# A second convolution in column halves, with three gate buffers in the room of a closed stage

## The chip, the cores and the metric

The kernel runs on one core of one Trainium2 chip. The metric is the device time of one launch in microseconds (us). Lower is better. A profiled execution leaves a trace, whose span runs from its first to its last instruction.

## What is computed

The input x is 2 images of 256 channels by 64 x 64, in fp32. Two layers follow each other.

```python
# layer 0: attention over all 4096 positions, 8 heads of 32 channels, and a mask
q, k, v = 1x1 convolutions of x
fuse    = softmax(q k^T / sqrt(32)) v
x       = (Wf [x; fuse] + bf) * m + x * (1 - m)
# layer 1: channel gate, window attention, spatial gate
x = x * sigmoid(relu(x ca_w1 + b) ca_w2 + b)
x = x + window_attention(x)            # windows of 8 x 8, 4 heads
x = x with its 256 channels shuffled (4 groups)
y = relu(bn1(conv7x7(x, sa_w1)))       # 64 groups: 4 channels in, 1 out
y = bn2(conv7x7(y, sa_w2))             # 64 groups: 1 channel in, 4 out
out = x * sigmoid(y)
```

The change is in the last convolution and in the gate after it.

## The kernel before

**Prologue.** Pools mk, w0, st0, x0 and cw (line 372) hold masks, weights, staging tiles, all of x and the convolution weights while q, k and v are projected and written to memory. v comes last: a matmul from x0 (line 470), a copy into a tile vst of st0 (478), two stores by POOL (483).

**Attention.** `pipeline` walks through 1024 slots of 128 keys. For each slot, `scores` multiplies k and q (631) and lets ScalarE (ACT) write exp into a tile e (641); `products` multiplies v and e on TensorE (PE, 660) and adds e up on VectorE (DVE, 662). k and v are loaded by SyncE (SP) in pieces (558, 560), two ahead, behind q (565) at the start; x and the mask for the first stage follow them (571, 574). Everything else is hung into these slots: `later` and `stages` hold steps with due times, and `stage(b, c)` does the rest of layer 0 and the window attention for 8 image rows, step by step, up to the rows xs in memory (980), which the convolution reads. The order of all engines is the order of the program (`manual_schedule`).

**Pools.** `arm` opens f, x, g and w (the stages' tiles) first, then `pipeline` opens conv, e (8 tiles e of 8 KB a partition and 3 sums of 8 KB), and kv and q, one after the other from the same end of the on-chip memory. kv and q are closed when the last slot is done, and a pool "late" takes their room. f, x, g and w stay open to the end.

**Convolution.** A 7 x 7 convolution is done as 7 matmuls over shifted columns d, with the rows of a block and their neighbours on the partitions, and banded weights that are prepared in memory. Rows are cut into three blocks (line 43) of up to 30. Four groups of channels make a unit u; there are 16 units. `items` (989) are 24 pieces of work: units 0 to 7 of image 0, units 2 to 7 of image 1, units 8 to 15 of both images at once, and units 1 and 0 of image 1. Items with one image have 3 x 64 = 192 columns, those with both 384. For item k,

- `conv1(k)` (1037) multiplies 4 x 7 times: all 128 rows, 32 weight columns for each of four groups (c1, 1046), then ReLU on ACT into y (1054);
- `conv2(k)` (1061) takes 32 rows of y, one strip for each j, with 128 weight columns, 4 x 7 times (c2, 1070). Its four results lie in two PSUM tiles of two banks, of which there are three in all. ACT takes tanh into z (1080) and z/4 + 1/4 (1086);
- `gate(k)` (1089) multiplies z by x on DVE (1092) and stores it: 12 stores for each image (1105), half from POOL and half from SP; items 4 to 7, after the stages, from POOL alone; the last item from ACT and SP. Then SP loads the rows of item k + 4 (1025) and the next weights (1018).

`convolve` hands items out in the order conv1(k + 1), conv2(k), gate(k), as a generator. The first ones are drawn while the last stage runs: `next(conv)` comes between its steps (1206 to 1209). Then `staged` is set, and the rest runs by itself. z has two buffers, each for two images (1077), from the pool "late".

The weights of c2 are `w[r, d]` from a view "p (m d) -> p d m": neighbouring columns stand 7 elements, 28 bytes, apart. A matmul on fp32 appears in the profile as two instructions, with a weight load each.

Of the kernel before, what the change touches and what calls it, by code (L numbers as in the profile page):

```python
# [10 lines left out]
F32 = mybir.dt.float32  # L11
# [6 lines left out]
B, C, H, W = 2, 256, 64, 64  # L18
N = H * W
P = 128  # L20
# [17 lines left out]
KS, PAD = 7, 3  # L38
# [2 lines left out]

RB = 30
BLOCKS = ((0, 0, 24), (17, 24, 40), (34, 40, 64))
NG = C // 4
UG = 4
UQ = UG // 4
NU = NG // UG
UW = UG * KS
# [7 lines left out]
def conv_seq_kernel(ctx: ExitStack, tc: tile.TileContext, a, out):  # L56
    nc = tc.nc
# [13 lines left out]
    def psum2(name):  # L71
        return ps["pair"].tile([P, 2, CH], F32, tag="s", name=name)
# [48 lines left out]

    x_s = dram.tile([B, len(BLOCKS), P, NG, WP], F32, name="xs")

# [42 lines left out]
    def prepare(mk, cwp):  # L166
# [19 lines left out]
        rows = 32 + 4  # L186
        bn1 = cwp.tile([rows, NG, 5], F32, name="bn1")
        nc.gpsimd.dma_start(
            bn1, a["bn1"].rearrange("g s o -> (g s o)").partition_broadcast(rows)
        )  # L190
        raw1 = cwp.tile([rows, NG, KS], F32, name="raw1")
        src = a["sa_w1"].rearrange("(h g) k (y x) -> h k y g x", h=2, y=KS)
# [20 lines left out]
        for i in range(4):  # L213
            for j in range(4):
                nc.gpsimd.dma_start(
                    raw2[KS * j : KS * j + KS, :, i, :], src[i % 2, i // 2, j]
                )
        m1 = cwp.tile([rows, NG, KS], F32, name="m1")
        nc.gpsimd.memset(m1, 0.0)
# [5 lines left out]
        for b in range(B):  # L225
            for n, r in ((0, 0), (len(BLOCKS) - 1, 31)):
                for q in range(4):
                    nc.gpsimd.dma_start(
                        x_s[b, n, 32 * q + r].rearrange("(p g) w -> p (g w)", g=2),
                        zero[0 : NG // 2, 0 : 2 * WP],  # L230
                    )
# [140 lines left out]
    with (  # L372
# [48 lines left out]
        for i, (b, c) in enumerate(chunks):  # L421
            load_chunk()
            x = xs0[i]
            sq = st0.tile([P, 2 * KC, CH], F32, tag="sq", name=f"sq_{b}_{c}")
            tops = st0.tile([P, 2 * KC, CH // 4], F32, tag="top4", name=f"top4_{b}_{c}")
            for n, w in (("q", wq), ("k", wk)):
                s = psum2(f"{n}0_{b}_{c}")
                for g in range(KC):
                    for kc in range(KC):
                        rhs = x[:, kc, :]  # L430
                        if n == "q":
# [5 lines left out]
                            start=(kc == 0),  # L437
                            stop=(kc == KC - 1),
# [26 lines left out]
        for i, (b, c) in enumerate(chunks):  # L465
            s = psum2(f"v0_{b}_{c}")
            sv = s.rearrange("p a (t o) -> p (a t) o", t=2)
            for m in range(4):
                for kc in range(KC):
# [4 lines left out]
                        start=(kc == 0),  # L474
                        stop=(kc == KC - 1),
# [21 lines left out]
            elif i == 2:  # L497
# [3 lines left out]
                for oc in range(KC):  # L501
                    for kc in range(KC):
# [4 lines left out]
                            start=(kc == 0),  # L507
                            stop=(kc == KC - 1),
# [11 lines left out]


    def pipeline(arm, shifted, pools):
        fp, xpool, gp, wp, avp, ctx_conv = pools
        cpool = ctx_conv.enter_context(tc.tile_pool(name=f"conv{arm}", bufs=1))

        ep = ctx_conv.enter_context(tc.tile_pool(name=f"e{arm}", bufs=EB))
# [1 line left out]
        att = ExitStack()  # L528
# [193 lines left out]
        def stage(b, c):  # L722
# [241 lines left out]
            for oc in range(KC):  # L964
# [4 lines left out]
                )  # L969
                for n, (x0, _, _) in enumerate(BLOCKS):  # L970

# [16 lines left out]

        items = [(u, (0,)) for u in range(EARLY)] + [(u, (1,)) for u in range(2, EARLY)]
        items += [(u, (0, 1)) for u in range(EARLY, NU)] + [(1, (1,)), (0, (1,))]  # L990
        staged = []

        def convolve():
            nb = len(BLOCKS)

# [13 lines left out]
            def load_w(u):  # L1009
                if u >= NU:  # L1010
                    return
                n = 2 * 32 * UW
                if u == 0:
                    t = cpool.tile([P, n], F32, name=f"w{arm}{u}")
                else:
                    t = ep.tile([P, HG, CH], F32, tag="e", name=f"w{arm}{u}")
                    t = t.rearrange("p h n -> p (h n)")[:, 0:n]
                nc.sync.dma_start(t, w_s[u])
                ws[u] = t
# [41 lines left out]
            def conv2(k):  # L1061
                u, images = items[k]
                n = nb * len(images)
                y = ys.pop(k)
                w = ws[u][:, 32 * UW :].rearrange("p (m d) -> p d m", d=KS)
                tiles = [psum2(f"c2{arm}{k}_{hh}") for hh in range(2)]
                for d in range(KS):
                    for j in range(4):
                        r = slice(32 * j, 32 * j + 32)
                        nc.tensor.matmul(  # L1070
                            tiles[j // 2][:, j % 2, 0 : n * W],
                            w[r, d],
                            y[r, 0:n, d : d + W],
                            start=(d == 0),
                            stop=(d == KS - 1),
                        )
                z = pool.tile([P, 4, B * nb * W], F32, tag="z", name=f"z{arm}{k}", bufs=2)
                z = z[:, :, 0 : n * W]
                for hh in range(2):
                    nc.scalar.activation(  # L1080
                        z[:, 2 * hh : 2 * hh + 2, :],
                        tiles[hh][:, :, 0 : n * W],
                        AF.Tanh,
                        scale=0.5,
                    )
                nc.scalar.activation(z, z, AF.Copy, bias=0.25, scale=0.25)  # L1086
                return z.rearrange("p j (n x) -> p j n x", x=W)

            def gate(k, z):
# [10 lines left out]
                for m, b in enumerate(images):  # L1100
                    for n, (x0, r0, r1) in enumerate(BLOCKS):
                        for i in range(4):
# [20 lines left out]
            load_rows(3)  # L1123
            load_w(0)
            pool = yield
            for _ in range(4):
                load_w(weights.popleft())
            conv1(0)
            yield
            for k, (u, images) in enumerate(items):  # L1130
                while len(xs) <= k + 1 < len(items):
                    if not more():
                        yield
                conv1(k + 1)
                yield
                more()
                z = conv2(k)
                yield
                more()
                gate(k, z)  # L1140
                if xcs or k + 4 < EARLY:
                    load_rows(k + 4)

                if weights and (weights[0] <= 1 + EB or k >= EARLY):
                    load_w(weights.popleft())
# [25 lines left out]
        for i, (b, c, g, m) in enumerate(slots):  # L1171
            now[0] = i
            if (b, c, g, m) == (B - 1, NCHUNK - 1, 0, 0):
                for _ in banded:
                    pass
                conv = convolve()
                next(conv)
            if m % PB == 0:
                load_piece(i // PB + AHEAD)
            if g == KC - 1 and m == 0:  # L1180
                nxt = (b, c + 1) if c + 1 < NCHUNK else (b + 1, 0)
                if nxt[0] < B:
                    load_q(*nxt)
            rest = scores(i + 2) if i + 2 < len(slots) else None
            products(i)
            if rest:
                rest()
            if g == KC - 1 and m == NMB - 1:
                late = EB + 5 if (b, c) == (0, 0) else 0
                at(DN + 6 + late, lambda b=b, c=c: stages.append(stage(b, c)))  # L1190
            run_later()
            if i % 5 == 1:
                next(banded, None)
            if i % 4 == 0:
                run_stages()
# [11 lines left out]
        while stages:  # L1207
            if run_stages():
                next(conv)
        staged.append(True)  # L1210
        for _ in conv:
            pass
        psum.close()
# [1 line left out]

    def arm(name, shifted):
        with (
            tc.tile_pool(name=f"f{name}", bufs=1) as fp,
            tc.tile_pool(name=f"x{name}", bufs=1) as xpool,
            tc.tile_pool(name=f"g{name}", bufs=1) as gp,  # L1220
            tc.tile_pool(name=f"w{name}", bufs=1) as wp,
            tc.tile_pool(name=f"av{name}", bufs=1, space=PSUM) as avp,
            ExitStack() as ctx_conv,
            tc.manual_schedule(),
        ):
            pipeline(name, shifted, (fp, xpool, gp, wp, avp, ctx_conv))

    safe = nc.values_load(flag[0:1, 0:1], min_val=0, max_val=1)
    with tc.If(safe > 0) as cond:
        arm("a", False)  # L1230
    with cond.Else():
        arm("b", True)
# [65 lines left out]
```

## Time and profile before

Three runs took 3001.16, 3001.5 and 3005.74 us. The page of the profiled execution has these numbers; its own time beside the span is not given.

| | |
|---|---|
| median of the runs | 3001.5 us |
| span of the profiled execution | 3002.6 us |
| PE busy | 2969.7 us (99%) |
| DVE busy | 2502.6 us (83%) |
| ACT busy | 2480.2 us (83%) |
| POOL busy | 267.0 us (9%) |
| c2: matmul instructions, mean | 1344, 438 ns |
| c2: matmul busy | 100.2 us |
| first and last c2 | 2779.7 and 2988.2 us |
| stores of the output by POOL | 210 of 569 ns |
| ACT's first activation of z waiting for stores | 69.2 us in all |

Busy time is the time in which an engine has at least one instruction running, so that matmuls side by side count once. PEld is the load of weights, which overlaps matmuls. "SPq" is the issue of a DMA by SyncE. The idle time that a line names is that of the engine just before the instruction, and the arrow shows what ended it.

### The profile page before, as it was taken

Reading aid. Unit: us, or ns where it says so; the run is one execution under the profiler, and the core shown is the slowest. Engines: PE = TensorE matmul, PEld = TensorE weight load, DVE = VectorE, ACT = ScalarE, POOL = GpSimd, SP = SyncE. Lnnn points to the kernel's source line nnn. Section 1 sums busy time; section 2 is a strip of 40 time slices with the busy share of each in tenths; the row PEclk is TensorE's granted clock in tenths of the full one; section 3 lists DMA queues with packets and bytes.
Section 4 is the critical chain, followed back from the end, with each engine's and each line's share of the span. In section 5 each row is a group of like instructions: output and inputs, shape, how many; then the busy total and the mean of one; then the engine's idle time right before and its main releaser. Section 6 shows DMA issues by size and latency. Waiting matters only on the chain.

```text
span 3002.6 us, 61009 instructions
## 1 busy us (share of the span) xinstructions
PE 2969.7 (99%) x25226; PEld 1016.9 (34%) x25226; DVE 2502.6 (83%) x1348; ACT 2480.2 (83%) x4151; POOL 267.0 (9%) x470
## 2 busy tenths in 40 slices
PE   9999999999999999999999999999999999999997
PEld 3552323222223222223222222322222222223775
DVE  3349999899999999998999999999999899999211
ACT  5569889898989898988989898989898898988433
POOL 8010000000000000000000000000000000000356
PEclk9999999999999999999999999999999999999999
DMA  8544321222242323232222222222323222422464
GB/s 245 201 172 159 119 69 52 77 64 71 55 77 62 80 59 80 62 70 69 67 68 64 69 58 71 62 71 61 78 65 71 68 68 67 106 62 82 143 194 105
DMA packets 223951, 266.03 MB, mean 89 GB/s; under 512 B 113384, under 2 KB 130108, under 8 KB 223408
## 3 DMA queue, kind: packets, MB, share of 16 engines
q1 hardware_dynamic: 200880, 231.47, 26.8%
q0 software_dynamic: 18416, 27.87, 4.6%
q8 instruction: 201, 3.29, 0.5%
q10 hardware_dynamic: 4368, 2.70, 0.3%
q14 instruction: 86, 0.70, 0.1%
HBM read 213.49 MB, written 66.13 MB: 93 GB/s over the span
## 4 chain that ended last, share of the span: by engine, by line
PE 95%; DVE 2%; DMA 1%; POOL 1%; ACT 1%; SPq 0%; issue 0%; DVEq 0%; ACTq 0%; POOLq 0%
PE sa L631 36%; PE ava L660 33%; PE qka L804 4%; PE hya L733 4%; PE c2a L1070 2%; PE q L433 2%; PE vwa L890 2%; PE k L433 2%; PE opa L954 2%; PE c1a L1046 2%; PE v L470 2%; DVE suma L662 1%; PE dna L683 1%; POOL out_dram L1105 1%; PE sca L838 1%; DMA out_dram<-za 1%
## 5 line engine op out<-in xcount | busy, mean ns | idle before, releaser
L662 DVE TENSOR_TENSOR suma<-suma,ea 128x2048 f32<-128x2048 f32 x960 | 2199.0, 2291 | 87.9 <-ACT ea L641 1.8
L641 ACT ACTIVATE ea<-sa 128x512 f32<-128x512 f32 (+1 forms) x3072 | 2044.4, 744 | 89.0 <-PE sa L631 38.0
L631 PE MATMUL sa<-qa,ka 32*128 32x512 f32 x8192 | 1191.9, 639 | 1.5 <-ACT vst L478 1.2
L660 PE MATMUL ava<-ea,va 128*32 128x512 f32 x8192 | 1091.1, 605 | 0.3 <-ACT fa L670 0.3
L631 PEld LDWEIGHTS sa<-qa,ka 32*128 32x128 f32 x8192 | 338.6, 183 | 755.7 <-ACT ea L641 686.3
L660 PEld LDWEIGHTS ava<-ea,va 128*32 128x32 f32 x8192 | 161.5, 108 | 779.0 <-issue 752.1
L980 POOL DMA_DIRECT2D xs<-xo x94 | 65.9, 708 | 2541.1 <-DVE xo L965 2540.9
L1105 POOL DMA_DIRECT2D out_dram<-za x210 | 117.8, 569 | 80.2 <-DVE za L1092 56.5
L804 PE MATMUL qka<-ua,qkv_w 128*128 128x512 f32 x256 | 118.4, 605 | 0.0
L1092 DVE TENSOR_TENSOR za<-za,xla 128x768 f32<-128x768 f32 (+1 forms) x16 | 21.7, 1359 | 113.6 <-ACT za L1086 82.5
L662 DVE TENSOR_TENSOR suma<-ea,ea 128x2048 f32<-128x2048 f32 x32 | 73.1, 2284 | 51.3 <-ACT ea L641 51.3
L1070 PE MATMUL c2a<-yca,wa 32*128 32x192 f32 (+1 forms) x1344 | 100.2, 438 | 7.5 <-ACT za L1080 7.5
L1080 ACT ACTIVATE za<-c2a 128x384 f32<-128x384 f32 (+1 forms) x48 | 26.2, 595 | 95.5 <-DMA out_dram<-za 69.2
L452 DVE TENSOR_REDUCE top<-sq 128x512 f32<-128x2048 f32 x16 | 36.6, 2286 | 79.8 <-ACT sq L446 79.8
L741 ACT ACTIVATE ta<-hya,bf 128x512 f32<-128x512 f32 x32 | 20.3, 684 | 95.3 <-PE hya L733 89.2
L1070 PEld LDWEIGHTS c2a<-yca,wa 32*128 32x128 f32 x1344 | 91.3, 315 | 18.2 <-issue 9.6
L859 ACT ACTIVATE ewa<-ewa,mxwa 128x64 f32<-128x64 f32 x256 | 85.2, 346 | 1.5 <-DVE mxwa L850 1.5
L817 ACT ACTIVATE qka<-qka,qkv_b 128x512 f32<-128x512 f32 x64 | 40.5, 683 | 41.8 <-PE qka L804 41.6
L745 DVE TENSOR_TENSOR ta<-ta,mca 128x512 f32<-128x512 f32 x32 | 22.1, 689 | 62.9 <-ACT ta L741 62.9
L804 PEld LDWEIGHTS qka<-ua,qkv_w 128*128 128x128 f32 x256 | 46.0, 189 | 71.3 <-issue 46.1
L433 PE MATMUL q<-x,WqT 128*128 128x512 f32 x128 | 61.7, 627 | 5.4 <-DMA WqT<-in_WqT_dram 5.4
L890 PE MATMUL vwa<-qkv_w,ua 128*128 128x256 f32 x256 | 59.5, 386 | 0.0
(137 smaller groups left out, 1516.8 us busy)
## 6 DMA issues: line engine op xcount, KB each, us to landing
ka<-ks SPq DMA_DIRECT2D x256, 256.0 KB
va<-vs SPq DMA_DIRECT2D x256, 256.0 KB
wa<-ws SPq DMA_DIRECT2D x17, 896.0 KB
ws<-zeros SPq DMA_DIRECT2D x16, 896.0 KB
xs<-xo POOLq DMA_DIRECT2D x78, 140.0 KB, 6.5
xla<-xs SPq DMA_DIRECT2D x24, 420.0 KB
x<-in_x_dram SPq DMA_DIRECT2D x16, 512.0 KB
qs<-qst SPq DMA_DIRECT2D x16, 512.0 KB
```

Source lines behind the costliest of these rows:

```text
L433: nc.tensor.matmul(s[:, g, :], w[:, kc, g * P : (g + 1) * P], rhs, start=(kc == 0), stop=(kc == KC - 1),)
L631: nc.tensor.matmul(heads[j], k[r, cols], q[r, g, :], start=True, stop=not shifted)
L641: nc.scalar.activation(e[:, h, :], tile, AF.Exp, scale=SCALE0)
L660: nc.tensor.matmul(av[r, :], v[:, m % PB, r], e[:, j, :], start=start, stop=stop)
L662: nc.vector.tensor_add(total, first[0] if m == 1 else total, e)
L733: nc.tensor.matmul(s[:, oc, :], wf[:, kc, oc * P : (oc + 1) * P], f[:, kc - KC, :] if half else xw[kc], start=(kc == 0), stop=(kc == 2 * K ...
L804: nc.tensor.matmul(s[:, j, :], wqkv[:, kc, o : o + P], u[:, kc, :], start=(kc == 0), stop=(kc == KC - 1),)
L859: nc.scalar.activation(e[:, n, :], e[:, n, :], AF.Exp, bias=mx[:, n : n + 1], accum_out=rs[:, n : n + 1],)
L890: nc.tensor.matmul(sv[:, t, :], u[:, kc, t * P : (t + 1) * P], wqkv[:, kc, 2 * C : 3 * C], start=(kc == 0), stop=(kc == KC - 1),)
L980: eng.dma_start(x_s[b, n, p + r0 : p + r1].rearrange("r g w -> g r w"), xo[64 * h : 64 * h + 64, oc, r0 - WS * c : r1 - WS * c, :],)
L1070: nc.tensor.matmul(tiles[j // 2][:, j % 2, 0 : n * W], w[r, d], y[r, 0:n, d : d + W], start=(d == 0), stop=(d == KS - 1),)
L1105: engines[stores % len(engines)].dma_start(dst[b, i, r0:r1, UG * u : UG * u + UG, :], z[p + r0 : p + r1, :, nb * m + n, :],)
```

## The change

The stationary operand of c2 is split into two halves of 64 columns. Each half is a matmul of its own, into the lower or upper 64 partitions of the same PSUM bank, with the same moving columns of y.

The four pools of the stages are opened on the right side of the memory, in the same order, and the others on the left without them below. When the last stage is done they are closed, and a pool "gate" is opened there. z has three buffers. While stages run it is taken from "late", with room for one image; after that from "gate", with room for two.

```diff
+HALVES = (slice(0, 64), slice(64, 128))
...
-        staged = []
+        staged, zpool = [], []
...
                 for d in range(KS):
                     for j in range(4):
                         r = slice(32 * j, 32 * j + 32)
-                        nc.tensor.matmul(
-                            tiles[j // 2][:, j % 2, 0 : n * W],
-                            w[r, d],
-                            y[r, 0:n, d : d + W],
-                            start=(d == 0),
-                            stop=(d == KS - 1),
-                        )
-                z = pool.tile([P, 4, B * nb * W], F32, tag="z", name=f"z{arm}{k}", bufs=2)
+                        for o in HALVES:
+                            nc.tensor.matmul(
+                                tiles[j // 2][o, j % 2, 0 : n * W],
+                                w[r, d, o],
+                                y[r, 0:n, d : d + W],
+                                start=(d == 0),
+                                stop=(d == KS - 1),
+                            )
+                size = B * nb * W if staged else nb * W
+                z = zpool[-1].tile([P, 4, size], F32, tag="z", name=f"z{arm}{k}", bufs=3)
...
             pool = yield
+            zpool.append(pool)
...
         staged.append(True)
+        stg.close()
+        zpool.append(att.enter_context(tc.tile_pool(name=f"gate{arm}", bufs=1, side="right")))
         for _ in conv:
             pass
...
         with (
-            tc.tile_pool(name=f"f{name}", bufs=1) as fp,
-            tc.tile_pool(name=f"x{name}", bufs=1) as xpool,
-            tc.tile_pool(name=f"g{name}", bufs=1) as gp,
-            tc.tile_pool(name=f"w{name}", bufs=1) as wp,
+            ExitStack() as ctx_conv,
+            ExitStack() as stg,
             tc.tile_pool(name=f"av{name}", bufs=1, space=PSUM) as avp,
-            ExitStack() as ctx_conv,
             tc.manual_schedule(),
         ):
-            pipeline(name, shifted, (fp, xpool, gp, wp, avp, ctx_conv))
+            held = [stg.enter_context(tc.tile_pool(name=f"{n}{name}", bufs=1, side="right")) for n in "fxgw"]
+            pipeline(name, shifted, (stg, *held, avp, ctx_conv))
```

More of the change, by code (lines that the diff above doesn't have):

```diff
@@ L522, in pipeline @@
     def pipeline(arm, shifted, pools):
-        fp, xpool, gp, wp, avp, ctx_conv = pools
+        stg, fp, xpool, gp, wp, avp, ctx_conv = pools
         cpool = ctx_conv.enter_context(tc.tile_pool(name=f"conv{arm}", bufs=1))
```

## The prediction

> **What bounds the kernel now.** I read the page first. Its shares of busy time give PE 99%, and its chain of work that ended last is 95% PE, of which the second convolution (c2a, L1070) is 2% and the first (c1a, L1046) 2%. So the change touches only the last 8% of the span, and the rest of this reading is from there: first the groups by shape, then the chain over the last 200 us, then the timeline.
>
> ```profile
> L1070 PEld LDWEIGHTS c2a<-yca,wa 32*128 32x128 f32 x1344 | 91.3, 315 | 18.2 <-issue 9.6 <-ACT za L1080 8.0
> L1046 PEld LDWEIGHTS c1a<-xla,wa 128*32 128x32 f32 x896 | 35.0, 139 | 21.1 <-issue 18.2 <-ACT za L1080 0.4
> L932 PEld LDWEIGHTS oa<-pta,vwa 64*64 64x64 f32 x1024 | 16.4, 134 | 12.8 <-ACT ea L641 12.6 <-issue 0.2
> L631 PEld LDWEIGHTS sa<-qa,ka 32*128 32x128 f32 x8192 | 338.6, 183 | 755.7 <-ACT ea L641 686.3 <-issue 62.4
> ```
>
> The columns are line, engine, operation, tiles, shape, count, busy us, mean ns of one, idle before. Weight loads of 128 columns take 183 ns where the columns lie side by side (L631) and 315 ns in the second convolution, whose weights stand 7 elements apart.
>
> ```profile
> 2870.49 4.78 DMA out_dram<-za
> ...
> 2883.45 3.49 PE c2a L1070 x55
> 2886.94 2.48 PE c1a L1046 x54
> 2889.42 3.51 PE c2a L1070 x56
> ...
> 2905.94 4.89 PE c2a L1070 x56
> 2910.83 4.76 PE c1a L1046 x52
> ```
>
> This is the chain in order of time (start, us, what). 56 instructions are 14 groups of four that run side by side. With one image (192 columns) a group of c2 costs 3.51/14 = 251 ns, a group of c1 2.48/14 = 177 ns, though both stream the same 192 columns: c2 waits for its weights. With two images (384 columns) it is 349 against 340 ns: there streaming covers the loads.
>
> ```profile
> 2826.22 1.16 PE L932 MATMUL oa<-pta,vwa 64*64 64x64 f32 x64
> 2854.42 12.73 POOL L1105 DMA_DIRECT2D out_dram<-za  x23 [0.53 <-DMA out_dram<-za]
> 2868.18 5.12 POOL L1105 DMA_DIRECT2D out_dram<-za  x9 [1.03 <-issue]
> 2875.26 0.87 ACT L1080 ACTIVATE za<-c2a 128x384 f32<-128x384 f32 x2 [9.63 <-DMA out_dram<-za]
> 2875.81 4.87 PE L1070 MATMUL c2a<-yca,wa 32*128 32x192 f32 x52 [4.94 <-ACT za L1080]
> 2984.46 0.87 ACT L1080 ACTIVATE za<-c2a 128x384 f32<-128x384 f32 x2 [5.07 <-DMA out_dram<-za]
> 2992.61 0.87 ACT L1080 ACTIVATE za<-c2a 128x384 f32<-128x384 f32 x2 [6.40 <-DMA out_dram<-za]
> ```
>
> In the timeline the bracket is the idle time and what ended it. Between 2833 and 2887, and again after 2976, the two gate buffers bound the work: POOL alone stores z4 to z7 (12 stores of 0.56 us each, 6.7 us an item, against 2.48 + 3.51 = 5.98 us that PE needs), ACT waits for a free z, PE waits for ACT's PSUM.
>
> ```profile
> 137.34 0.38 SPq L558 DMA_DIRECT2D ka<-ks  x1
> 190.27 0.38 SPq L571 DMA_DIRECT2D xa<-in_x_dram  x1
> 185.97 1.07 POOL L483 DMA_DIRECT2D vs<-vst  x2 [2.38 <-ACT vst L478]
> 187.10 8.35 ACT L641 ACTIVATE ea<-sa 128x512 f32<-128x512 f32 x13
> ```
>
> This is the seam between prologue and attention. The x load stands in SP's queue from 139 to 190.27. It overlays no tile that is still in use, only pools of the prologue; what it waits for is the last v store from st0 (issued by 187.04, 3.2 us to land). So a new pool waits here for the whole pool that held its room.
>
> [...] No row here shows eight, but L932 shows four of 64x64: 64 instructions in 1.16 us, 72 ns for a group of four. c1 streams a column in 177/192 = 0.92 ns, so 64 columns take 59 ns, and two column halves in turn would take 118. So column halves of the same rows do run together. [...] 139 (32 columns) and 315 (128), both strided, agree: about 80 + 1.84 per column. The second part alone, 128 x 1.84 = 235 ns, is nearly the 251 of a group; for 64 columns it is 118, under the 177 that streaming takes (an estimate from these rows).
>
> **The change part by part.** The sum stands against the span of 3002.6 us; the page gives no other time of that execution, and it is 1.1 us over the median of 3001.5. I take the difference to the median.
>
> *Two halves of 64 columns.* Each of the 24 items now issues 112 matmuls and 112 loads instead of 56. c1 is the nearest row: strided loads, four column tiles on the same rows, the stream the bound. I take c1's 2.48 plus 0.07 for eight starts instead of four: 2.55 us with one image (saves 0.96), 4.79 with two (saves 0.1; bounds 0 and 0.13). Lower bound 2.48, upper bound 3.51 if loads of two halves take turns. Issue: the densest 10 us of the trace (2819 to 2829) holds 566 PE instructions, 17.7 ns each; c1 + c2 would need 5.03 us/336 = 15.0 ns.
>
> *Items 0 to 3* (2779 to 2833): three z of half the size bring nothing, as ACT waits there for PE and never for a store. They lie in PE's order between the last stage's steps. 4 x 0.96 = 3.8; c2(1) hides the gating multiply (ends 2800.15, next matmul 2801.00), 0.85 us of cover against 0.96, so 3.7 remains. The others keep over 1 us.
>
> *Items 4 to 13, with three buffers* (c2(4) starts at 2833.4; times from there). Before, c2(11) ends at 53.5 and c2(13) at 67.7. Now c2(k) would end at 2.55 + 5.03(k-4). POOL's queue starts 1.0 us earlier and keeps its pace: z5 stored by 21, z6 by 27.8, z7 by 35.5 (36.5 before). z8 takes z5's buffer: no wait (c2(8) ends 22.7). z9 takes z6's: landed 29.5, c2(9) ends 27.7, PSUM covers it. z10 takes z7's: landed 37.2, or 40.8 if x and weight loads of 1.3 MB again go before it, as now (2869.9 stored, 2875.3 free). c2(11) waits for that and ends at 40 to 43.8, I take 43. Then c1(13), c2(12), c1(14), c2(13): 2.48 + 2.55 + 4.76 + 2.55, and 0.9 for rows of item 14, which are loaded only after gate(10): 56. Gain 11.7 (10.6 to 14.3).
>
> *Items 14 to 20*: PE bound, 7 x 0.1 = 0.7.
>
> *The end* (from the end of c2(20), 2968.6; the span ends at 34.0). z22 and z23 no longer wait for z20 and z21. c2(23) ends at 15.4 instead of 20, its gate at 18.8. What is late next is POOL: its 30 stores of z20 to z22 end at 24.25 now, and depend on nothing that gets faster; SP's 36 have idle time between them. Number and order of stores and loads on both queues stay as they were. 24.3 + 2.6 to land + 1.6 of closing steps (as after SP's last store, 2998.4 to 3001.0 to 3002.6) = 28.5. Gain 5.5, up to 7.7 if POOL's idle 2.2 us at 2979.4 goes.
>
> *Pools on the other side.* No view shows places; they follow from the shapes in the order of opening, in KB above the constants. The prologue: st0 9.6 to 54.6, x0 54.6 to 120.2, cw to 138.5. Before: stage pools 0 to 48.8, conv to 72.8, e with sum to 162.9, then k and v (beyond everything: loaded at 137). Now, with the stage pools on the right: conv 0 to 24.0, e and sum 24.0 to 114.1, k and v 114.1 to 126.4. So k and v wait for x0, which the v projection reads until 184.6, and e waits for st0, which is free at 190.2. SP holds the first k load back to 185, and behind it two v, one k, x and mask, of which only k matters at once; it takes 3 to 4.8 us to land (4.8 at 137), so the scores start at 188 to 190. ACT's first exp, with all of ACT behind it, starts at 190.3 to 191.2 instead of 187.10. PE follows ACT there (0.26 us wait at 189.10). Cost 3.2 to 4.2, I take 3.8. If tiles and not pools are waited for, k still lands at 188: 1.5 to 2. The gate pool's own wait is free: its room is last read at 2835.5, z4 is written at 2836.0.
>
> Sum: 3.7 + 11.7 + 0.7 + 5.5 - 3.8 = 17.8 us; 3001.5 - 17.8 = 2983.7.
>
> **The rivals.** (a) *No faster c2*: loads of two halves take turns, or 17.7 ns an instruction is the floor (336 x 17.7 = 5.95 us, as now). Only the buffers work: 8.0 from items 4 to 13 (c2(11) ends at 45.5), 5.5 at the end, less 3.8: 9.7, 2991.8. For: no row with eight tiles. Against: c1's four strided loads fit in 177 ns. (b) *Slower*: the halves of one row strip stream in turn, since they read the same y rows. A group takes 354 ns with one image and 680 with two, c2 4.95 and 9.5 us: items 0 to 3 lose 5.8, 4 to 13 6, 14 to 20 33, the start 3.8, the end nothing: about 3049. It decides from 251 + 9.7/224 groups = 294 ns on. Against: L932. (c) *Nothing*: the third buffer is eaten, since POOL's store queue sets z10 as it set z9, and the end waits for it too; 3.7 less 3.8: 3001.
>
> **How the numbers follow.** Forecast 0.64 (2976 to 2989, the ends from 2.48 us for c2, 14.3, 7.7 and a start of 2 us, and from the late ends of each); (a) 0.20 (2988 to 2995); (b) 0.09; (c) 0.07. The range 2976 to 2995 leaves out (b), (c) and tails. A measurement can tell 0.2% (6 us) from no change: faster 0.84, within 0.07, slower 0.09.
>
> **What would show it.** c2 with 192 columns in about 2.55 us, with 384 in 4.8; the first exp near 190.5 and the first k load near 185; ACT's waits for out_dram of 69.2 us down below 25; c2(23) never short of PSUM for over 1 us; the last POOL store about 24 us after c2(20), and the span ending 4 us later. A c2 of 3.5 us means (a), of 5 (b). If the end still waits on ACT for z, the reading of the third buffer is wrong.

## The result, and the profile after

The change made no difference that can be measured: 3002.42 us (median of 13 runs, 2999.57 to 3006.38) against 3002.29 us (13 runs, 3000.41 to 3005.74) for the kernel before, ratio 1.0, 95% interval 0.9992 to 1.0008. The profiled execution of the changed kernel took 2999.62 us, its span 2997.8 us. So the two profiled spans differ by 4.8 us where the medians differ by 0.1; the 13 runs of a kernel lie up to some 4 us from their median. What follows sets the two traces side by side. Lines have moved by one to four: c2 is L1072, c1 L1047, the tanh into z L1083, the stores L1108, the load of rows L1026, the exp L642.

The second convolution did become faster. First the groups by shape of the changed kernel, then its chain of waits.

```profile
L1072 PEld LDWEIGHTS c2a<-yca,wa 32*64 32x64 f32 x2688 | 64.2, 191 | 20.5 <-issue 10.6 <-ACT za L1083 1.3
```

```profile
2804.13 2.64 PE c2a L1072 x112
...
2817.24 2.57 PE c2a L1072 x112
...
2886.30 5.60 DMA xla<-xs
2891.90 0.14 issue
2892.03 6.98 PE c1a L1047 x55
...
2906.34 4.80 PE c2a L1072 x112
```

A load of 64 strided columns takes 191 ns, between the 139 of 32 and the 315 of 128; the prediction's 80 + 1.84 per column, an estimate from those two shapes, gives 198. c2 takes 2.57 us with one image (3.51 before) and 4.80 with two (4.89). But c1 of item 14 now stands in the chain behind a load of rows, and takes 6.98 us where the same work took 4.76.

The table gives the time of each stretch in the two traces, in us; a start is that of the first instruction, an end the start of the last one (the prediction's ends lie some 0.3 us later, which the differences leave out). Each difference is rounded by itself.

| stretch | before | after | difference | predicted |
|---|---|---|---|---|
| start to c1(0) | 2771.9 | 2779.4 | +7.5 | +3.8 |
| c1(0) to c2(4), items 0 to 3 | 61.5 | 59.8 | -1.7 | -3.7 |
| c2(4) to the end of c2(11) | 53.1 | 42.8 | -10.3 | -10.5 |
| on to the end of c2(13) | 14.2 | 19.2 | +5.0 | -1.2 |
| on to the end of c2(20) | 67.4 | 66.6 | -0.7 | -0.7 |
| on to the end of the span | 34.5 | 29.9 | -4.6 | -5.5 |
| sum | | | -4.8 | -17.8 |

The largest loss is at the start. This is the chain there, then what the view of the tile vst says on who waited for it, then the DMA issues between 183 and 196 us (KB each, median us to landing), and the windows (busy us of PE, PEld, DVE, ACT and POOL, then PE's granted clock, DMA share, GB/s).

```profile
185.62 0.53 POOL vs L484
186.15 0.48 DMA vs<-vst
...
186.84 6.23 issue
...
193.32 0.61 ACT ea L642
193.92 0.04 issue
193.97 3.96 PE sa L632 x10
197.93 1.86 PE ava L661 x8
```

```profile
  ACT ea L642: 6.5, 1
```

```profile
vs<-vst POOLq DMA_DIRECT2D x3, 256.0 KB, 6.1
ka<-ks SPq DMA_DIRECT2D x3, 256.0 KB
```

```profile
190.00:192.00 2.00, 0.75 (x3) 0.00 (x0) 0.00 (x0) 0.00 (x0) 0.00 (x0) 0.50 1.04 390
```

The first exp starts at 193.32 instead of 187.10. It waits for the last v store, which reads vst in st0: issued by 186.69, landed at 193.0. Before, such a store landed in 2.5 us (median of the same view of the kernel before); now 6.1, while the first loads of k, v, x and the mask, held back to 184.27, run at the same time and the DMA engines are full (share 1.04). PE stands still for 2.72 us before its first scores and for 3.22 us after them; its clock is 0.50 from 186.4 to 200.1.

After the stages the gate buffers bound less, but other stops show. In PE's timeline, c1 and c2 stop in the middle of their own matmuls, with nothing to wait for that the profile shows; in SP's, six stores of gate(10) go ahead of the load of the rows of item 14.

```profile
2832.16 2.20 PE L1047 MATMUL c1a<-xea,wa 128*32 128x192 f32 x46
2834.80 0.87 PE L1047 MATMUL c1a<-xea,wa 128*32 128x192 f32 x10 [0.43 <-issue]
...
2852.43 2.21 PE L1047 MATMUL c1a<-xla,wa 128*32 128x192 f32 x44
2855.82 0.88 PE L1047 MATMUL c1a<-xla,wa 128*32 128x192 f32 x12 [1.17 <-issue]
...
2892.03 6.98 PE L1047 MATMUL c1a<-xla,wa 128*32 128x384 f32 x56 [4.60 <-DMA xla<-xs]
```

```profile
2881.99 3.31 SPq L1108 DMA_DIRECT2D out_dram<-za  x6
2885.36 2.33 SPq L1026 DMA_DIRECT2D xla<-xs  x2
```

```profile
2888.00:2892.00 4.00, 0.00 (x0) 0.00 (x0) 0.96 (x1) 1.11 (x2) 4.00 (x8) 0.72 0.97 299
2892.00:2894.00 2.00, 1.97 (x16) 0.76 (x20) 0.00 (x0) 0.00 (x0) 0.64 (x2) 0.50 0.98 339
...
2898.00:2900.00 2.00, 2.00 (x64) 1.25 (x63) 0.00 (x0) 0.59 (x1) 0.00 (x0) 1.00 0.95 372
```

PE waits 4.60 us for the rows; in these windows its clock falls to 0.50 while it stands still, and it computes half of c1(14) at that. So the wait costs 4.6 us and 2.2 more (6.98 - 4.76): the clock is 0.50 from 2889.8 to 2896.6, which is some 4.5 us of the work behind the wait. What a stop costs in clock differs from run to run: in experiments below, stops of 2.50 us (halves where they pay, c2(3)) and 1.85 us (loads first, c2(11)) were each followed by 3.4 us at 0.50, one of 2.40 us (SP shares items 6 and 7, c2(11)) was not. The kernel before paid in clock as well, behind its own stop of 4.94 us: 0.50 from 2874.5 to 2881.3. So here this cost moved; it is not new.

ACT's waits for a free z are less, and at the very end PE and ACT no longer matter (timelines of ACT and of POOL):

```profile
2879.23 0.87 ACT L1083 ACTIVATE za<-c2a 128x384 f32<-128x384 f32 x2 [6.19 <-DMA out_dram<-za]
...
2980.70 0.87 ACT L1083 ACTIVATE za<-c2a 128x384 f32<-128x384 f32 x2 [1.66 <-PE c2a L1072]
...
2985.47 0.87 ACT L1083 ACTIVATE za<-c2a 128x384 f32<-128x384 f32 x2 [3.02 <-DMA out_dram<-za]
```

```profile
2857.56 14.10 POOL L1108 DMA_DIRECT2D out_dram<-za  x25 [0.21 <-issue]
```

z10 still waits 6.19 us for POOL's stores (4.1 of it after c2(10) has ended), z22 for nothing but PE, z23 for 3.02 us; POOL keeps its 0.56 us a store.

### The profile page after: what moved, and what is told of

Read it like the earlier page. It is cut to its first block, busy times and chain, and to the rows that moved or that the text cites. A ratio compares the mean times of both kernels' runs of the same rounds, so it can differ in the third digit from the quotient of the medians.

```text
span 2997.8 us, 63638 instructions
## 1 busy us (share of the span) xinstructions
PE 2958.7 (99%) x26570; PEld 990.8 (33%) x26570; DVE 2501.2 (83%) x1348; ACT 2480.8 (83%) x4151; POOL 267.1 (9%) x470
## 3 DMA queue, kind: packets, MB, share of 16 engines
q1 hardware_dynamic: 200880, 231.47, 27.3%
## 4 chain that ended last, share of the span: by engine, by line
PE 93%; DVE 2%; POOL 2%; DMA 1%; ACT 1%; issue 1%; SPq 0%; ACTq 0%; DVEq 0%
PE sa L632 36%; PE ava L661 34%; PE qka L805 4%; PE hya L734 4%; PE vwa L891 2%; PE opa L955 2%; PE v L471 2%; PE q L434 2%; POOL out_dram L1108 2%; PE k L434 1%; PE c1a L1047 1%; PE c2a L1072 1%; PE dna L684 1%; DVE suma L663 1%; PE sca L839 1%; DMA out_dram<-za 1%
## 5 line engine op out<-in xcount | busy, mean ns | idle before, releaser
L642 ACT ACTIVATE ea<-sa 128x512 f32<-128x512 f32 (+1 forms) x3072 | 2044.7, 744 | 96.5 <-PE sa L632 39.0
L1108 POOL DMA_DIRECT2D out_dram<-za x210 | 117.8, 569 | 72.3 <-DVE za L1095 44.4
L1072 PE MATMUL c2a<-yca,wa 32*64 32x192 f32 (+1 forms) x2688 | 83.0, 383 | 1.2 <-ACT za L1083 0.7
L1083 ACT ACTIVATE za<-c2a 128x384 f32<-128x384 f32 (+1 forms) x48 | 26.1, 595 | 68.9 <-DMA out_dram<-za 45.3
L1072 PEld LDWEIGHTS c2a<-yca,wa 32*64 32x64 f32 x2688 | 64.2, 191 | 20.5 <-issue 10.6
L1047 PE MATMUL c1a<-xla,wa 128*32 128x192 f32 (+1 forms) x896 | 62.1, 422 | 7.1 <-DMA xla<-xs 5.7
```

Of the source, the lines that this page charges most:

```text
L642: nc.scalar.activation(e[:, h, :], tile, AF.Exp, scale=SCALE0)
L1047: nc.tensor.matmul(s[32 * j : 32 * j + 32, 0 : n * W], w[:, j, d, :], xs[k][:, 0:n, j, d : d + W], start=(d == 0), stop=(d == KS - 1),)
L1072: nc.tensor.matmul(tiles[j // 2][o, j % 2, 0 : n * W], w[r, d, o], y[r, 0:n, d : d + W], start=(d == 0), stop=(d == KS - 1),)
L1108: engines[stores % len(engines)].dma_start(dst[b, i, r0:r1, UG * u : UG * u + UG, :], z[p + r0 : p + r1, :, nb * m + n, :],)
```

## The experiments

**The theory** after this comparison (S): the gain in the convolution is real, and the moved pools take nearly all of it back at the start. **The rival** (D): after the stages the transfers bound whatever PE and ACT do, so halves and buffers gain next to nothing, and the start is noise. The parts were therefore run alone. "late" holds three full z buffers, so the third buffer needs no moved pools. All medians below stand beside runs of the kernel before on the same chip (medians 3002.05 to 3003.19).

| kernel | us | ratio to before, 95% interval |
|---|---|---|
| the change | 3002.4 | 1.0 (0.9992 to 1.0008) |
| halves and three buffers, pools unmoved | 2993.6 | 0.9969 (0.9958 to 0.9981) |
| three buffers alone | 2995.3 | 0.9978 (0.9969 to 0.9987) |
| halves alone | 3000.3 | 0.9995 (0.9988 to 1.0001) |
| moved pools alone | 3010.5 | 1.0025 (1.0016 to 1.0035) |
| the change, waits by tile | 2996.3 | 0.9985 (0.9975 to 0.9994) |
| quarters | 3057.5 | 1.0185 (1.0169 to 1.0201) |
| loads first | 2994.0 | 0.9972 (0.9962 to 0.9983) |
| loads first, SP shares items 4 to 7 | 2998.6 | 0.9989 (0.9980 to 0.9997) |
| loads first, SP shares items 6 and 7 | 2993.8 | 0.9967 (0.9955 to 0.9979) |
| loads first, halves in 0 to 3 and 20 to 23 | 2994.0 | 0.9971 (0.9960 to 0.9982) |
| the same, item 3 whole | 2991.1 | 0.9960 (0.9947 to 0.9974) |

### The parts alone

Halves and three buffers, from the kernel before:

```diff
-                z = pool.tile([P, 4, B * nb * W], F32, tag="z", name=f"z{arm}{k}", bufs=2)
+                z = pool.tile([P, 4, B * nb * W], F32, tag="z", name=f"z{arm}{k}", bufs=3)
...
+                        for o in HALVES:
+                            nc.tensor.matmul(
+                                tiles[j // 2][o, j % 2, 0 : n * W],
+                                w[r, d, o],
```

> The kernel before, with c2 in column halves and three gate buffers, all from the pool 'late'; the pools of the stages stay where they were. Theory S (the gain is real, and the seam between prologue and attention eats it): the first exp is back at 187, the start costs nothing, and what the profile of the changed kernel showed after 2770 us is kept: about 7 us less than the changed kernel, 2995. Rival D (the convolutions have become bound by transfers, so nothing is gained in most runs): the same as before, 3002, with or without the pools.

Three buffers alone, the first two lines of that diff:

> The kernel before with three gate buffers alone. Theory S: no start cost, 8 us in items 4 to 13 and 4.5 to 5.5 at the end, if row loads do not take part of it back: 2990 to 2996. Rival D: 3002, since POOL's stores and the loads set the pace and not the buffers.

Halves alone, the rest of it:

> The kernel before with the column halves alone, two gate buffers. Theory S: 2 to 3 us from items 0 to 3 [...], 0.7 from the items of two images, little from items 4 to 13, which wait for z: 2997 to 3000. Rival D: 3002.

Moved pools alone: the changed kernel with whole tiles of 128 columns and `bufs=2`:

> The pools of the change alone: stages on the right, the gate pool in their room, two buffers, c2 with 128 columns. Theory S: the first exp at 193 and the first c1 7 us later, nothing gained afterwards: 3009. Rival D: within 2 us of before, if attention makes up for a late start.

Measured: moved pools +8.2 us, three buffers -7.0, halves -2.0, halves and buffers together -8.7. The parts add up: -8.7 + 8.2 = -0.5, against +0.1 for the whole change. The rival is out, since the buffers alone gain 7.0 us, with an interval well below 1. What the halves add is not clear of the noise, alone (the interval reaches 1.0001) or on top of the buffers (1.7 us, in intervals that overlap). With the pools unmoved the first exp comes right behind the table load (1.28 us from 184.99) and a first activation of 0.20 us (timeline of ACT, halves and three buffers, pools unmoved); with the pools moved and nothing else it comes at 194.49, after the same wait.

```profile
186.40 13.88 ACT L642 ACTIVATE ea<-sa 128x512 f32<-128x512 f32 x21
```

```profile
194.49 3.90 ACT L642 ACTIVATE ea<-sa 128x512 f32<-128x512 f32 x6 [6.43 <-issue]
```

### Waits by tile instead of by pool

```diff
-        ep = ctx_conv.enter_context(tc.tile_pool(name=f"e{arm}", bufs=EB))
+        ep = ctx_conv.enter_context(tc.tile_pool(name=f"e{arm}", bufs=EB, reuse_waits="tile"))
...
+        kvp = att.enter_context(tc.tile_pool(name=f"kv{arm}", bufs=AHEAD + 1, reuse_waits="tile"))
+        qp = att.enter_context(tc.tile_pool(name=f"q{arm}", bufs=2, reuse_waits="tile"))
```

> The change whole, with one thing altered: the pools e, kv and q wait for the tiles whose room they take over, not for whole pools. My theory: the 8.2 us that the moved pools cost lie at the seam, and come from two waits that a pool adds: k, v and x loads are held back until 184 and then run together with the last v store, and ACT's first exp waits until 193.0 for that store. With waits by tile the exp needs no more than k landed: first exp between 187.5 and 190, and the time 3 to 6 us below the change's 3002.4, 2996 to 2999.5. Rival: the seam's cost is not the pools' waits but the k load itself, which has to come after x0 is read anyway: first exp 190 to 193, time 3000 to 3002.5. Second rival: the 8.2 us do not lie at the seam at all; then the first exp comes early and the time stays at 3002.

2996.3 us: 6.1 less than the change by the medians, 4.5 by the ratios to the kernel before (1.8 to 7.5 by the interval), and the first exp starts at 188.96. In its chain k is loaded no earlier (184.60), but nothing waits for the last v store any more:

```profile
184.60 2.76 DMA ka<-ks
187.36 0.14 issue
187.50 5.13 PE sa L632 x23
```

So more than half of the 8.2 us, about three quarters by the medians, are waits of whole pools. The three pools were altered together; that it is e's wait for st0 above all is read from the trace, where k comes no earlier. The other 2.7 us, against the kernel with unmoved pools, go with k's late load: there the exp starts 2.6 us earlier.

### More, shorter matmuls

Quarters, from halves and three buffers with the pools unmoved:

```diff
-HALVES = (slice(0, 64), slice(64, 128))
+HALVES = tuple(slice(32 * i, 32 * i + 32) for i in range(4))
```

> Halves with three gate buffers from the pool late (2993.6), with four tiles of 32 columns in place of two of 64: each c2 issues 224 matmul instructions and 224 weight loads, for the same streaming. Theory that PE's instruction supply limits short matmuls (14 to 15 ns an instruction where the stalls of the change lie): c1 + c2 of one image are 560 instructions, 7.8 to 8.4 us instead of 5.0, in 14 items, and about 9.1 us (16 ns each) in the ones with two images: 3 us lost in items 0 to 3 each, 2 to 3 in 4 to 13: 3015 to 3035, with stalls at block boundaries all through. Rival, no limit of supply, the stalls had another cause: c2 stays at 2.5 to 2.6 us (bound by streaming), time 2993 to 2995.

3057.5 us, 64 more than with halves, and more than expected. Two things show in its trace. From the start of the first to the start of the last instruction, an undisturbed c2 takes 3.85 us instead of 2.32 with one image, and 5.93 instead of 4.39 with two, with no gap in it: 1.54 us, or 110 ns a group, which I had left out; 24 times that is 37 us. The other 27 us I put down to gaps like those of the changed kernel, and to the clock behind them, which is 0.50 in six stretches of 27.3 us in all (one of 3.4 us with halves); how they divide was not separated. Twelve gaps of 1.3 to 3.5 us lie between 2841 and 2950 alone (22.3 us together; here and below a gap is counted from the start of one matmul to that of the next, some 0.3 us more than the idle time in a bracket). Every one is at the same place: in the single records of PE, at the 194th or 195th instruction of a block of 256 (PE's instructions counted from the start), called the block boundary below. With halves the gaps stand at this number too (four in the changed kernel, 0.77, 0.76, 1.50 and 0.52 us); the kernel before and the two with whole tiles alone have none. A 16 KB transfer of the instruction queue ends 1.2 to 1.5 us before each gap of the changed kernel ends. That kernel's page counts 211 of these transfers, with 53140 instructions of PE and PEld; the page before counts 201, with 50452. The changed kernel's DMA view from 2875 to 2905 lists five:

```profile
q8 instruction: 5, 0.08, 1.1%
```

That PE runs out of instructions there, called the supply of instructions below, is inferred from this; that the gaps depend on the number of instructions is tested by the last two runs.

### Loads ahead of stores

From halves and three buffers, pools unmoved:

```diff
                 nc.vector.tensor_mul(z, z, x.rearrange("p n g x -> p g n x"))
+                load_next(k)
...
-                if xcs or k + 4 < EARLY:
-                    load_rows(k + 4)
...
```

`load_next` holds the lines taken out, rows and weights.

> Halves with three gate buffers from the pool late (2993.6), with SP's loads of the next rows and weights issued ahead of the item's own stores instead of after them. Theory that the wait for the rows of item 14 is SP's order (six stores of 3.3 us in all ahead of the load): the rows come 3 us earlier, the wait of c1(14) goes from 3 to 5 us down to under 1.5 us, time 2989.5 to 2992. Rival, the DMA engines are full there (0.9 of their time) and the order only changes who waits: the wait moves to z, or stays; 2993 to 2995.

2994.0 us, the rival's number, but not for its reason. c1(14) no longer waits, and takes 4.80 us; the time is lost at block boundaries again, in c2(3) and c2(11) above all (PE's timeline):

```profile
2819.64 2.30 PE L1072 MATMUL c2a<-yca,wa 32*64 32x192 f32 x94
2824.97 0.91 PE L1072 MATMUL c2a<-yca,wa 32*64 32x192 f32 x18 [3.02 <-issue]
```

```profile
2874.60 2.23 PE L1072 MATMUL c2a<-yca,wa 32*64 32x192 f32 x82
2878.69 0.97 PE L1072 MATMUL c2a<-yca,wa 32*64 32x192 f32 x30 [1.85 <-issue]
...
2886.28 4.80 PE L1047 MATMUL c1a<-xla,wa 128*32 128x384 f32 x56
```

Why c2(3) now stops longer can be read from the DMA records. In the kernel with loads last PE passed the block boundary before this one at 2818.75, and the 16 KB transfer started at 2819.85. Here PE passes it at 2819.01, and the transfer starts at 2822.74. These are the two stretches, first that with loads last (columns as in the windows above):

```profile
2818.75:2819.85 1.10, 1.10 (x70) 1.03 (x69) 0.00 (x0) 0.43 (x2) 1.10 (x3) 1.00 0.48 96
```

```profile
2819.01:2822.74 3.73, 2.93 (x143) 2.57 (x135) 0.00 (x0) 1.11 (x2) 1.49 (x3) 1.00 1.01 354
```

The next rows and weights are issued at 2816.59 and 2817.03 instead of 2818.89 and 2819.33, so the DMA engines are full (share 1.01) in the 3.73 us before the transfer starts. At the boundaries on either side of this one the engines are idle, and the transfer starts 0.47 and 1.13 us after PE has passed. So two things go with a gap here: PE is through a block in little time (278 instructions in 2.93 us of busy time in the second stretch), and the DMA engines are full while the next block is due.

### SP shares the stores of items 4 to 7

```diff
-                elif staged and k < EARLY:
-                    engines = (nc.gpsimd,)
```

> The kernel with loads first, and SP also takes every second store of items 4 to 7, which POOL stored alone. Theory that POOL's store queue holds z10 back (its 12 stores of 0.56 us an item against 5.0 us that PE needs): c2(11) ends at 38 to 40 us after c2(4) starts, instead of 42.8, time 2 to 4 us below the kernel with loads first. Rival, the transfers share the same engines and set the pace, not their issue: c2(11) stays at 42 to 43, or what it gains is lost again at the rows of item 14; same time within 1 us.

2998.6 us, slower than either expected. PE was through c2(20) 1.2 us earlier, and z10 waited for no store (its tanh starts as c2(10) ends), so POOL's queue is what holds z10 back. But after its last store POOL's closing DRAIN instruction took 10.26 us, in single records from 2984.19 to 2994.45, where it takes 2.34 in ten other kernels here, the kernel before among them; SP had seen all stores landed by 2988.2. Why is open. A smaller shift avoided it:

```diff
-                elif staged and k < EARLY:
+                elif staged and k < EARLY - 2:
```

> The kernel with loads first (2994.0), with SP taking every second store of items 6 and 7 only, instead of all of 4 to 7 (2998.6). There z10 no longer waited for a store and PE was through c2(20) 1.2 us earlier, but POOL's closing drain took 10.26 us instead of 2.34. Theory: POOL's queue delays z10, and half of the shift is enough: z10 waits under 1.5 us, c2(20) ends 0.5 to 2 us earlier than with loads first; if the closing drain is 2.3 us, 2991.5 to 2993.5. Rival: any store taken from POOL brings the long drain, 2998 to 2999; second rival: the transfers, not their issue, delay z10, then 2994.

2993.8 us, the second rival's number. z10 waited for no store here either, and the drain took 1.36 us; c2(11) and c2(12) stopped for 2.72 and 2.27 us at block boundaries, and c2(20) ended no earlier. What the freed buffer gave here, these stops took.

### Halves only where they pay

```diff
-                        for o in HALVES:
+                        for o in HALVES if k < 4 or k >= 20 else (slice(0, P),):
```

> The kernel with loads first (2994.0), with halves only in items 0 to 3 and 20 to 23; items 4 to 19 have whole tiles of 128 columns again. Theory that PE's instruction supply runs short where c1 and halved c2 follow each other without a pause: items 4 to 13 of the kernel with loads first lose 1.11, 1.08, 1.07 and 2.17 us at block boundaries, and these gaps are gone here, while the streams of items 4 to 13 take 0.96 us each longer; c2(11) ends 43 to 46 us after c2(4) starts, and the time stays within 1.5 us of 2994. Rival: the gaps are not from the number of instructions (then they stay, at other places, and the time goes up by 4 to 8 us, 2998 to 3002).

2994.0 us, although two thirds of the items have whole tiles again. Between c2(4) and c1(14) PE has no gap at all (its timeline):

```profile
2863.72 3.57 PE L1072 MATMUL c2a<-yca,wa 32*128 32x192 f32 x56
2867.21 2.54 PE L1047 MATMUL c1a<-xla,wa 128*32 128x192 f32 x56
2869.69 3.58 PE L1072 MATMUL c2a<-yca,wa 32*128 32x192 f32 x56
2873.19 2.54 PE L1047 MATMUL c1a<-xla,wa 128*32 128x192 f32 x56
```

c2(11) ends 45.0 us after c2(4) starts, seven items of 5.97 and a c2 of 3.2, bound by PE alone; with halves in all items it was 45.0 too, and the whole way to c2(13) takes 59.2 us here and 59.0 there. With halves in all items there were gaps of 1.11, 1.08, 1.07 and 2.17 us in items 4 to 13; with fewer instructions and the same transfers they are gone. One gap is left, of 2.82 us in c2(3), and it costs clock as well (timeline and window of PE):

```profile
2824.36 0.81 PE L1072 MATMUL c2a<-yca,wa 32*64 32x192 f32 x18 [2.50 <-issue]
2825.11 1.64 PE L933 MATMUL oa<-pta,vwa 64*64 64x64 f32 x64
2826.67 3.62 PE L1047 MATMUL c1a<-xea,wa 128*32 128x192 f32 x56
```

```profile
2826.00:2828.00 2.00, 2.00 (x48) 1.39 (x46) 0.96 (x1) 2.00 (x3) 0.00 (x0) 0.50 0.00 0
```

c1(5) takes 3.62 us where a c1 takes 2.54. This gap was the subject of the last run:

```diff
-                        for o in HALVES if k < 4 or k >= 20 else (slice(0, P),):
+                        for o in HALVES if k < 3 or k >= 20 else (slice(0, P),):
```

> The kernel with halves in items 0 to 3 and 20 to 23 alone (2994.0), with item 3 whole too. In every kernel with loads first, c2(3) stands still for 2.8 to 3.7 us at a block boundary of PE's instructions, in the middle of its matmuls. Theory that 112 instructions more in c2(3) make the supply run short there: with 112 instead of 224 instructions the gap goes or shrinks below 1 us, against 0.96 us more of streaming; c2(4) starts 1 to 2 us earlier, time 2992 to 2993. Rival: the fetch of that block comes late for a reason that has nothing to do with c2(3) (the queue, or another transfer); the gap stays at the same block, and the time rises by up to 1 us, 2994 to 2995.

2991.1 us, the lowest median here and some 1 us below the range expected, 0.9960 (0.9947 to 0.9974) of the kernel before; against the runs of the kernel before beside them, this one gains 10.9 us and the one above 9.2. The gap has shrunk and lies behind c2(3), at the same block, and the clock stays at 1.00 (PE's timeline):

```profile
2821.09 3.56 PE L1072 MATMUL c2a<-yca,wa 32*128 32x192 f32 x56
2824.58 0.81 PE L933 MATMUL oa<-pta,vwa 64*64 64x64 f32 x38
2825.79 0.62 PE L933 MATMUL oa<-pta,vwa 64*64 64x64 f32 x26 [0.41 <-issue]
```

The transfer of the block came no sooner: 3.07 us after PE passed the boundary before, with a DMA share of 1.03, against 3.14 us and 1.04 in the kernel above. What changed is that PE needs the block later, with 112 instructions fewer in c2(3).

## Why the prediction was wrong

It said 2983.7 us and faster; it came out as 3002.4 and the same. The gap is 18.7 us. In the traces 13.0 of it can be placed (17.8 predicted, 4.8 found); the other 5.7 lie between the traces and the medians. The changed kernel's trace is 2.8 us below its median; the median before is 3002.3 over 13 runs, not 3001.5. And a span is not a run's time: each of the 13 runs of the changed kernel took some 1.8 us more than its span. By that the traced execution of the kernel before took about 3004.4 us, 2.1 above its median (an estimate), where the prediction set the span against the median as if it were a run's time.

**Items 4 to 13 failed most, by 6.4 us, at the one wait put at 0.9.** Up to c2(11) the working held (its end 43.1 us after c2(4) starts, 43 predicted), through the wait of z10 for POOL. The rows of item 14 were known to be "loaded only after gate(10)", but SP's six stores of 3.3 us ahead of them and a landing in 5.6 to 6.5 us were not worked out: the wait was 4.6, and 2.2 at half clock came on top. Loads ahead of stores took both away, and lost as much again at block boundaries (2994.0 us in all, against 2993.6 with loads last).

**The seam failed by 3.7 us** (7.5 for the 3.8 taken; 8.2 with the pools moved alone). Its mechanism was right: k loaded from 184.27 ("back to 185"), and exp waiting for st0. What failed is "st0, which is free at 190.2": that was the landing of the last v store with the DMA engines to itself. The prediction moved the loads of k, v, x and the mask into these very microseconds and priced their landing, but not the store's, which went from some 3 to 6.3 us. The clock of 0.50 after the wait was not counted either: the first products are 7.2 us late, the exp 6.2.

**Items 0 to 3 failed by 2.0 us, by a cost put at nothing: gaps at block boundaries, read as the supply of instructions.** The prediction took 17.7 ns an instruction from a dense stretch, saw that 15.0 were needed, and went on; rival (a) named this floor. In the trace c2(3) and c1(5), where the gaps of 0.77 and 0.76 us lie, take 0.92 and 0.98 us longer than c2(2) and c1(4), which is 1.9 of the 2.0. 17.7 isn't a floor for one c2, which issues 224 instructions in 2.57 us, 11.5 ns each. Over some items something near it holds: from c2(4) to c2(9) the changed kernel needed 28.2 us for five times 336, 16.8 ns each. With the buffers and the rows right, halves gained nothing beyond whole tiles in items 4 to 13 (59.0 against 59.2 us from c2(4) to the end of c2(13)); that the same limit is why is inferred.

**The end failed by 0.9 us, in the closing steps.** POOL's last store ended 24.3 us after the end of c2(20), as predicted; from there to the end of the span it is 5.2 us, not 4.2, with POOL's own drain of 2.34 us in it. The claim that ACT's waits for stores would fall below 25 us was wrong (45.3 measured): 24.8 of them lie in the two-image items, where PE has work enough. c2(23) was not short of PSUM by over 1 us, as said (0.28 us of idle time before it, and 0.7 us longer than an undisturbed one); but z23 did wait for a store, 1.6 us past the end of c2(23), which the prediction had named as a sign against its reading of the third buffer. It cost nothing, as POOL's stores ended later.

**What held:** c2 at 2.55 and 4.79 us (2.57 and 4.80), and with it that eight tiles of 32x64 run together (184 ns for a group of eight, 177 for one of c1), which no view of before had shown (the 0.07 us for eight starts was my estimate); 0.7 us in items 14 to 20; no sign of rival (b). Of rival (c), "nothing gained", only the sum came true: its reason did not, as three buffers alone gain 7.0 us.

## What to carry to other kernels

The pools that were opened elsewhere waited here, as a whole, for what had held their new room (first exp 6.2 us later; 8.2 us for the moved pools alone). Where a pool moves, name the last reader of that room, and price that reader's transfer together with the loads that the move puts beside it. A PE wait of 4.6 us cost half as much again in clock, and one of 2.5 us cost 1.1. Where a change doubles PE's instructions, compare nanoseconds per instruction over a thousand and more of them (16.8 here), not over one burst (11.5), and split matmuls only where something else leaves PE time to take in more (in items 4 to 13 halves took 59.0 us and whole tiles 59.2). Look also at what fills the DMA engines there: the transfer for c2(3) began 3.73 us after PE had passed the boundary before with them full, and 1.10 us after with a share of 0.48.

## What was not expected of the hardware

- PE stood still for 0.5 to 3.7 us at the 194th or 195th instruction of a block of 256, where short matmuls follow each other for long; that its instructions ran short is inferred. The transfer of the next block started 3.73 us after PE had passed the boundary before where the DMA share was 1.01, and 0.47 us after where it was 0.00. That full engines hold it back is read from two kernels that differ in the order of loads and stores alone; it was not tried with less to transfer.
- Four tiles of 32 columns cost 110 ns a group more than two of 64, with 192 and with 384 columns alike, so it isn't streaming. Which part of loads or starts it is wasn't tried.
- The granted clock fell to 0.50 behind stops of PE of 1.85 us (loads first) and 2.50 us (halves where they pay), but not behind one of 2.40 us (SP shares items 6 and 7).
- POOL's closing drain took 10.26 us in one kernel and 1.36 to 2.42 in the others, with 24 stores fewer on POOL; with 12 fewer it did not.
